# Four gathers of 4 KB rows in place of one gather of 16 KB rows, in a chain of adapter and paged-attention layers

## The chip, the cores and the metric

The kernel runs on one core of one Trainium2 chip. The metric is the device time of one execution in microseconds (us). The five engines are called PE (TensorE), DVE (VectorE), ACT (ScalarE), POOL (GpSimd) and SP (SyncE); PEld is PE's loading of weights. POOL issues all indirect transfers (gathers and scatters); SP and ACT issue the plain ones.

## The reference

The input is 64 batches of 64 tokens with 512 features. Four residual layers follow one another:

```python
x = x + einsum('bct,bcd->bdt', x, weights[conditions])            # layer 0
x = x + x @ W_base.T + lora(x, adapter_idx)                       # layer 1
x = x + attention(x, k_blocks, v_blocks, block_tables, kv_lens)   # layer 2
x = x + x @ W.T + lora2(x, adapter_idx)                           # layer 3
```

Layer 2 matters here. It projects queries, keys and values, normalises and rotates queries and keys, writes the 64 new keys and values of each batch into blocks of a paged cache, and attends over a window of 256 positions:

```python
slot, off = pos // 16, pos % 16
blk = take_along_axis(block_tables, slot, axis=1)
k_blocks = k_blocks.at[blk, :, off, :].set(k)
v_blocks = v_blocks.at[blk, :, off, :].set(v)
k_all, v_all = k_blocks[block_tables], v_blocks[block_tables]
o = softmax(mask(q @ k_all.T * SCALE)) @ v_all
```

A block holds 16 positions, 4 key heads and 64 numbers for each: 4,096 floats, 16 KB. The block tables are drawn at random, so a batch may see blocks that another batch has written.

## The kernel before, in words

The work has two loops, and the order of all instructions is written out by hand: each engine runs its own in the order in which the program issues them.

The **first loop** (L879 on, 39 rounds) does layers 0 and 1 and the projections for tiles of 128 tokens. The new keys and values of each tile are scattered by POOL (`put_rows`, L831) into two tables in DRAM, `pk` and `pv`. These hold one row of 4,096 floats for each of the 5 blocks that a batch writes (64 x 5 = 320 rows); in a row the 16 positions come one after the other, each with 4 heads of 64. Before, the rows were filled with the old blocks, so that a row of `pk` is a whole block with the new tokens in it. Index lists are made in rounds 13 to 20: `ik_old` and `ik_new` for keys, `iv_old` and `iv_new` for values. An index of `ik_new` names the row of `pk` that a block of the window has become, or lies beyond the last row if nobody wrote that block; a gather skips such indices.

The **second loop** (L1117) has 128 steps, 8 to each group `q` of four batches; `i` is the step within the group, and each step does two key heads of one batch. A group's window is 21 blocks for each of four batches, so its keys stand on 84 partitions. They come about in four moves:

- `k_load` (L148): two gathers of old blocks into `kt`, 84 rows of 8 KB each, at steps 2 and 3, two groups ahead.
- `k_copy` (L154): four copies of `kt` into `k2`, which turns (head, position) into (position, head). Three of them run at steps 5 to 7, on DVE (ACT for the first two groups), the last on ACT at step 0.
- `k_patch` (L161): one gather from `pk` over `k2`, 84 indices, rows of 16 KB. It is issued at step 1 for the next group (L1130), and for group 0 at the end of the first loop (L896).
- `k_turn` (L169): PE transposes `k2` in eight turns of four (`psk` in the profile), one at step 3 and the others until step 7; ACT and DVE copy the outcome into `kT_mem`, from which the scores are made. A turn reads one position out of each quarter of the block: positions `o4`, 4 + `o4`, 8 + `o4` and 12 + `o4`.

Values go a like way: `v_load` (four gathers of 92 rows of 1 KB, in every even step), `v_copy` on ACT, `v_patch` (L199, one gather of 92 indices from `pv`, rows of 4 KB, in every odd step), and `v_share`, three small transfers on SP's queue that wait for the patch.

At a step POOL is given, in this order: at an odd step the value patch, then at step 1 the key patch; at an even step the four value loads; at steps 2 and 3 an old-key load. In the first 8 steps POOL also does the last multiplication of the remaining query tiles (`turned`, L218, the row L248), which PE transposes two steps later (`turn_q`, L276, `pst`). Where the first loop goes over to the second (round 32, L895 to L899) the order is: key patch of group 0, value patches of batches 0 and 1, then the multiplication of a query tile.

In the profile `k2` is named `k`, so the key patch is `k<-pk,ik_new`, the old-key load `kt<-in_kblk_dram,ik_old`, the value load `vs_mem<-in_vblk_dram,iv_old` and the value patch `vt_mem<-pv,iv_new`. All gathers are issued by the helper `gather` and have its line, L65.

Of the kernel before, what the change touches and what calls it, by code (L numbers as in the profile page):

```python
# [11 lines left out]
I32 = mybir.dt.int32  # L12
AF = mybir.ActivationFunctionType
ALU = mybir.AluOpType
# [4 lines left out]
P = 128  # L19
B, T, D = 64, 64, 512  # L20
# [3 lines left out]
NB_TAB = 257  # L24
# [7 lines left out]
NR = 21  # L32
NW = 5
W0 = NR - NW
NWR = B * NW
# [15 lines left out]
def kernel(  # L51
# [9 lines left out]
    V, S, G, PE, DMA = nc.vector, nc.scalar, nc.gpsimd, nc.tensor, nc.sync  # L61

    def gather(dst, src, idx, bound=None):
        more = {} if bound is None else dict(bounds_check=bound, oob_is_err=False)
        G.indirect_dma_start(  # L65
            out=dst, out_offset=None, in_=src,
            in_offset=bass.IndirectOffsetOnAxis(ap=idx, axis=0), **more,
        )
# [19 lines left out]
    pk = dram.tile([NWR, ROW], F32, name="pk", tag="pk")  # L88
# [4 lines left out]
    def ctile(shape, dt, name, pool=const):  # L93
        return pool.tile(shape, dt, name=name, tag=name)
# [14 lines left out]
    woT_sb = ctile([P, 4, D], F32, "woT_sb")  # L109
# [7 lines left out]
    edge = ctile([P, 1], F32, "edge")  # L117
    lowb = ctile([P, B], F32, "lowb")
    ik_old = ctile([4 * NR, 2, 16], I32, "ik_old")
    ik_new = ctile([4 * NR, 16], I32, "ik_new")  # L120
    iv_old = ctile([NV, B, NG], I32, "iv_old")
    iv_new = ctile([NV, B], I32, "iv_new")
    iod_f = iod.rearrange("p o q j -> p (o q j)")
# [8 lines left out]
    k2 = ctile([P, BLK, NG, HD], F32, "k2")  # L132
# [8 lines left out]
    def bank(pool, name):  # L141
        return pool.tile([P, 512], F32, name=name, tag="b")

    NP = 4 * NR
# [13 lines left out]
                k2[:NP].rearrange("p (oq o) g d -> p oq o g d", o=4)[:, :, o4],  # L158
                kt[:NP].rearrange("p g (oq o) d -> p oq o g d", o=4)[:, :, o4])

    def k_patch(q):  # L161

        if q < B // 4:
            gather(k2[:NP].rearrange("p o g d -> p (o g d)"), pk, ik_new[:, q : q + 1], NWR - 1)

    def kT(q, gp):
        return kT_mem[q % 2][:, gp].rearrange("p (b o c i) -> p b o c i", b=4, o=3, c=4)
# [31 lines left out]
    def v_patch(b):  # L199
        if b < B:  # L200
            gather(vt_mem[:NV, b % 4], pv.rearrange("w (q r) -> (w q) r", q=4),
                   iv_new[:, b : b + 1], NWR * 4 - 1)
# [11 lines left out]
    def queries(n):  # L214

        return n - LQ if n < NTILE - 4 else -1 if n < NTILE else n - 4 - LQ
# [77 lines left out]
    with ExitStack() as one:  # L294
# [4 lines left out]
        def t1(shape, dt, name):  # L299
            return ctile(shape, dt, name, c1)  # L300
# [41 lines left out]
                        for i in range(2))  # L342
        kvb_i = t1([P, B], I32, "kvb_i")
        kvp_i = t1([P, 1], I32, "kvp_i")
        cond_i = t1([P, B], I32, "cond_i")
        ad1_i = t1([P, B], I32, "ad1_i")
        ad3_i = t1([P, B], I32, "ad3_i")
        tab_i = woT_sb[:, 2, :NB_TAB].bitcast(I32)
        sc1b = t1([P, 4], F32, "sc1b")
        sc3b = t1([P, 8], F32, "sc3b")  # L350
        pcol = t1([P, 1], F32, "pcol")
# [212 lines left out]
        def gather_indices(part):  # L564

            ps = bank(psO, f"ps_idx{part}")
            lhs, rhs, m, n = ((ix["lhs"].rearrange("p b j -> p (b j)"), ix["hi"], 4 * NR, 16)
                              if part < 2 else
                              (ix["lhsv"].rearrange("p c i -> p (c i)")[:, :NV], ident2, NV, B))
            o = ps[:m, :n]  # L570
            PE.matmul(o, lhsT=lhs, rhs=rhs, start=True, stop=True)
            if part == 0:
                for h in range(2):
                    V.tensor_scalar(ik_old[:, h], o, 2.0, float(h), ALU.mult, ALU.add)
            elif part == 1:
                V.tensor_copy(ik_new, o)
            elif part == 3:
                V.tensor_scalar(iv_new, o, 4.0, ix["oq"], ALU.mult, ALU.add)
            else:
                for g in range(NG):  # L580
                    V.tensor_scalar(iv_old[:, :, g], o, 16.0, ix["oqg"][:, g : g + 1],
                                    ALU.mult, ALU.add)
# [299 lines left out]
        for n in range(NLAST):  # L882
# [10 lines left out]
                put_rows(done["p"])  # L893
                done["p"] += 1
            if n == NTILE:  # L895
                k_patch(0)  # L896
                v_patch(0)
                v_patch(1)
                norm_q(queries(n - 1))()  # L899
# [217 lines left out]
    for s, (q, b, gp) in enumerate(steps):  # L1117
        i = s % 8
        turn1, turn2 = turns.get(i, (None, None))
        if i == 0 and q:  # L1120
            x_load(q)
        if i == 2:
            q_load(q + 1)
        if gp == 0:
            v_load(b + 3)
        else:
            v_share(b + 1)
            v_patch(b + 2)
        if i == 1:
            k_patch(q + 1)  # L1130
        if i in (2, 3):
            k_load(q + 2, i - 2)
        scores(s + 1)
        turn_p(s)
        if 0 < s < 16:
            turn_q(nq + s - 2, psO)
        if turn1:
            k_turn(q + 1, *turn1)
        maxima(s + 1)
        keep_p(s)  # L1140
        exponentials(s + 1)
        second = norm_q(nq + s if q < 2 else -1)
        if parts:
            parts.pop(0)()
        if q < 2:
            product_q(nq + s + 1, psM)
            x2_load(nq + s + 3)
        shares(s + 1)
        second()
        if gp:  # L1150
            window(b + 2)
        po = values(s)
        if turn2:
            k_turn(q + 1, *turn2)
        keep_o(s, po)
        if gp == 0:
            v_copy(b + 2)
        if i == 0:
            k_copy(q + 1, 3)
        elif i > 4:  # L1160
            k_copy(q + 2, i - 5)
        if i == 7:
            parts += last_parts(q)
# [53 lines left out]
```

## Time and profile before

| what | us |
|---|---|
| median of 14 runs | 1233.82 |
| lowest and highest of them | 1220.99, 1244.74 |
| the profiled execution's own time | 1228.75 |
| its span, first to last instruction | 1227.0 |
| granted TensorE clock, mean | 0.979 |

The profile is of one execution. A busy time is the sum of an engine's instructions; issuing a plain transfer doesn't count as busy, but a gather's work on POOL does, and a transfer goes on in the DMA engines after POOL has done with it. A row of a timeline gives the start, the duration, the engine, the line, the operation with what it writes and reads, how many are merged, and in brackets how long the engine stood idle before and what ended that: an instruction of another engine, a transfer (DMA), or "issue", where nothing that the profile shows was waited for. The chain of waits follows back, from the last instruction, what each step was released by. The landing of a gather is read from the records of its semaphore, which counts the sixteen DMA engines that have finished their part; in the second loop some of these records are missing, so that a landing read there is the latest that is known.

### The profile page before, as it was taken

The page shows a single profiled execution, that of the slowest core. Times are in us where ns is not written, and L with a number is a line of the kernel's source. Part 1 is how long each engine was busy: PE and PEld are TensorE (multiplying, and loading weights), DVE is VectorE, ACT ScalarE, POOL GpSimd, SP SyncE. Part 2 cuts the span into 40 slices and gives each one's busy share as a digit, 9 for nine tenths or more (in the row PEclk, how much of TensorE's full clock was granted, in tenths as well). Part 3 has the DMA queues.
Part 4 walks back from the last instruction along what each step waited for, and adds up shares of the span by engine and source line. Part 5 has one row for each costly group of instructions (what it writes and reads, how often), then busy time and mean ns, then how long its engine had stood idle before and what let it go on. Part 6 is the DMA issues. An engine that isn't in the chain of part 4 may idle for free.

```text
span 1227.0 us, 17686 instructions
## 1 busy us (share of the span) xinstructions
PE 1103.7 (90%) x5622; PEld 636.9 (52%) x5622; DVE 755.4 (62%) x2313; ACT 571.7 (47%) x1472; POOL 612.3 (50%) x601
## 2 busy tenths in 40 slices
PE   4899899999999968978999998898999799999998
PEld 3434444444444434446555555655665555665565
DVE  3775346766666655885665665665666465666561
ACT  1332222232324324545665665565665465666651
POOL 3243323332642442887566656656666556665520
PEclk9999899999999988999999999999999899999999
DMA  8365713234331363636456645645656645755420
GB/s 268 133 250 209 237 41 113 90 97 132 113 110 47 108 181 110 167 93 153 133 134 142 148 121 129 155 120 124 163 134 136 142 120 126 157 143 143 98 64 35
DMA packets 129820, 163.20 MB, mean 133 GB/s; under 512 B 58079, under 2 KB 96891, under 8 KB 125545
## 3 DMA queue, kind: packets, MB, share of 16 engines
q0 software_dynamic: 63872, 85.04, 28.7%
q1 hardware_dynamic: 46416, 53.89, 14.5%
q10 hardware_dynamic: 19440, 23.15, 5.6%
q8 instruction: 45, 0.74, 0.3%
q14 instruction: 47, 0.39, 0.1%
HBM read 139.66 MB, written 50.33 MB: 155 GB/s over the span
## 4 chain that ended last, share of the span: by engine, by line
PE 68%; DVE 9%; issue 7%; DMA 6%; ACT 4%; POOL 2%; another core or an unknown queue 0%; ACTq 0%; POOLq 0%; DVEq 0%; SPq 0%
PE pso L1059 9%; PE pp L1025 8%; PE po L1041 7%; PE psc L983 7%; PE q L263 6%; PE ps L787 5%; PE kv L820 5%; PE psy L1084 4%; PE psy L1078 4%; PE psk L175 4%; PE psxa L1067 2%; PE psy L1086 2%; PE ps L789 2%; DMA pk<-vt_mem,zidx 1%; PE pst L283 1%
## 5 line engine op out<-in xcount | busy, mean ns | idle before, releaser
L65 POOL DMA_INDIRECT vs_mem<-in_vblk_dram,iv_old x256 | 310.5, 1213 | 77.4 <-issue 69.8
L65 POOL DMA_INDIRECT vt_mem<-pv,iv_new x64 | 80.1, 1252 | 168.1 <-ACT vt_mem L197 87.1
L1009 ACT ACTIVATE sm_mem<-sm_mem,mn 128x336 f32<-128x336 f32 x256 | 145.6, 574 | 32.9 <-DVE mn L999 28.4
L999 DVE CUSTOM_DVE_ANT_0 sm_mem<-psc,pen 128x336 f32<-128x336 f32 x256 | 119.5, 500 | 46.0 <-PE pp L1025 21.8
L1041 PEld LDWEIGHTS po<-pT,vt_mem 124*64 124x64 f32 x1536 | 84.5, 137 | 87.4 <-ACT sm_mem L1009 53.8
L1041 PE MATMUL po<-pT,vt_mem 124*64 124x128 f32 x1536 | 117.6, 282 | 13.1 <-issue 7.1
L1059 PE MATMUL pso<-oT,woT_sb 128*128 128x256 f32 x512 | 123.2, 385 | 0.0
L263 PE MATMUL q<-wq_sb,x2q 128*128 128x512 f32 x256 | 121.1, 618 | 0.0
L1025 PE MATMUL pp<-ident,sm_mem 128*124 128x128 f32 x768 | 115.0, 282 | 6.6 <-DVE rsum L1016 3.3
L820 PE MATMUL kv<-wkv_sb,xr 128*128 128x512 f32 x256 | 118.1, 606 | 0.4 <-ACT va L828 0.4
L983 PE MATMUL psc<-kT_mem,qs 64*128 64x336 f32 x512 | 108.0, 497 | 10.8 <-DVE kT_mem L184 9.7
L1025 PEld LDWEIGHTS pp<-ident,sm_mem 128*124 128x124 f32 x768 | 80.8, 139 | 70.7 <-issue 59.4
L787 PE MATMUL ps<-kT_mem,kT_mem 128*128 128x512 f32 x256 | 115.3, 593 | 0.6 <-PE ps_fill L493 0.6
L1017 DVE TENSOR_SCALAR sm_mem<-sm_mem,rsum 128x336 f32<-128x336 f32 x256 | 107.4, 420 | 9.1
L248 POOL TENSOR_TENSOR q<-q,rsq 128x512 f32<-128x512 f32 x30 | 31.4, 1048 | 138.8 <-DVE rsq L246 108.1
L1059 PEld LDWEIGHTS pso<-oT,woT_sb 128*128 128x128 f32 x512 | 92.5, 192 | 12.6 <-ACT pen L973 2.1
L175 PE MATMUL psk<-ident,k 84*128 84x84 f32 x512 | 63.8, 251 | 29.5 <-ACT kT_mem L184 13.6
L1032 DVE COPY pT<-pp 124x384 f32<-124x384 f32 x128 | 70.7, 552 | 18.6 <-PE pp L1025 6.8
L263 PEld LDWEIGHTS q<-wq_sb,x2q 128*128 128x128 f32 x256 | 50.1, 200 | 59.6 <-issue 59.4
L787 PEld LDWEIGHTS ps<-kT_mem,kT_mem 128*128 128x128 f32 x256 | 48.4, 190 | 60.5 <-issue 59.3
L820 PEld LDWEIGHTS kv<-wkv_sb,xr 128*128 128x128 f32 x256 | 47.9, 194 | 58.1 <-issue 56.4
L1032 ACT COPY pT<-pp 124x384 f32<-124x384 f32 x128 | 61.6, 482 | 34.1 <-PE pp L1025 25.4
(223 smaller groups left out, 1742.3 us busy)
## 6 DMA issues: line engine op xcount, KB each, us to landing
xt<-in_x_dram SPq DMA_DIRECT2D x32, 256.0 KB
x2d<-xr SPq DMA_DIRECT2D x8, 1024.0 KB
x2q<-x2d SPq DMA_DIRECT2D x32, 256.0 KB
qd<-qt ACTq DMA_DIRECT2D x64, 128.0 KB
qs<-qd SPq DMA_DIRECT2D x16, 512.0 KB
xq<-x2d SPq DMA_DIRECT2D x16, 512.0 KB
out_dram<-ys ACTq DMA_DIRECT2D x32, 256.0 KB
vt_mem<-vt_mem SPq DMA_DIRECT2D x192, 28.0 KB
```

Of the source, the lines that this page charges most:

```text
L65: G.indirect_dma_start(out=dst, out_offset=None, in_=src, in_offset=bass.IndirectOffsetOnAxis(ap=idx, axis=0), **more,)
L175: PE.transpose(ps[:, oq, :], k2[:NP, 4 * oq + o4, 2 * gp : 2 * gp + 2].rearrange("p g d -> p (g d)"), ident[:NP, :NP])
L263: PE.matmul(psq[n], lhsT=xt[:, c, :], rhs=wq_sb[:, c, :], start=(c == 0), stop=(c == KC - 1))
L787: PE.matmul(ps, lhsT=wb_sb[:, c, oc * P : (oc + 1) * P], rhs=x1_mem[:, c, :], start=(c == 0), stop=False)
L820: PE.matmul(pskv[n], lhsT=xrs[s][:, c, i * P : (i + 1) * P], rhs=wkv_sb[:, c, :], start=(c == 0), stop=(c == KC - 1))
L983: PE.matmul(pscs[s][g], lhsT=qts[q][gs, gp, b % 4].rearrange("p h t -> p (h t)"), rhs=kT(q, gp)[gs, b % 4].rearrange("p o c i -> p (o c i) ...
L999: V.tensor_tensor_reduce(rows4(sm)[:, :, :, :28], rows4(pscs[s][g]), rows4(pens[b]), SCALE, 3.0e38, ALU.add, ALU.min, mn)
L1009: S.activation(w, w, AF.Exp, bias=mn, scale=-1.0, accum_out=rsum)
L1025: PE.transpose(pp[:NVK, o, :], sms[s][g][0][:, o * P : o * P + NVK], ident)
L1032: (V.tensor_copy if g else S.copy)(pT, pps[s][g][:NVK])
L1041: PE.matmul(po[g * HD : (g + 1) * HD, :], lhsT=vt(b)[:NVK, o, 2 * gp + g], rhs=pTs[s][g][:, o, :], start=(o == 0), stop=(o == 2))
L1059: PE.matmul(o, lhsT=woT_sb[:, c, ec * P : (ec + 1) * P], rhs=oT[:, c // 2, :, c % 2, :], start=(c == 0), stop=(c == 3))
```

## The change

The gather of `k_patch` becomes four, each for a quarter of the 16 positions. `pk` is read as a table of 1,280 rows of 4 KB; the index of a quarter is four times the old index plus the quarter's number, and the bound is four times as large, so the same blocks are skipped. The index list grows from 16 to 64 numbers on a partition and is made by four DVE instructions in place of one. At both places the four are issued one after the other where the one stood. To make room, two index tables that are used only at the very start (`cond_i`, `ad1_i`) move into a part of `woT_sb` that is loaded later; another such table stood there already.

```diff
-    ik_new = ctile([4 * NR, 16], I32, "ik_new")
+    ik_new = ctile([4 * NR, 4, 16], I32, "ik_new")
...
-    def k_patch(q):
+    def k_patch(q, oq):
         if q < B // 4:
-            gather(k2[:NP].rearrange("p o g d -> p (o g d)"), pk, ik_new[:, q : q + 1], NWR - 1)
+            gather(k2[:NP, 4 * oq : 4 * oq + 4].rearrange("p o g d -> p (o g d)"),
+                   pk.rearrange("w (q r) -> (w q) r", q=4), ik_new[:, oq, q : q + 1], NWR * 4 - 1)
...
-        cond_i = t1([P, B], I32, "cond_i")
-        ad1_i = t1([P, B], I32, "ad1_i")
         ad3_i = t1([P, B], I32, "ad3_i")
-        tab_i = woT_sb[:, 2, :NB_TAB].bitcast(I32)
+        tab_i, cond_i, ad1_i = (woT_sb[:, 2, lo : lo + n].bitcast(I32)
+                                for lo, n in ((0, NB_TAB), (NB_TAB, B), (NB_TAB + B, B)))
...
             elif part == 1:
-                V.tensor_copy(ik_new, o)
+                for oq in range(4):
+                    V.tensor_scalar(ik_new[:, oq], o, 4.0, float(oq), ALU.mult, ALU.add)
...
             if n == NTILE:
-                k_patch(0)
+                for oq in range(4):
+                    k_patch(0, oq)
                 v_patch(0)
                 v_patch(1)
                 norm_q(queries(n - 1))()
...
         if i == 1:
-            k_patch(q + 1)
+            for oq in range(4):
+                k_patch(q + 1, oq)
```

## The prediction

> **What bounds the kernel now.** I read the page first, then the busy time by stage, then POOL's timeline around the gathers that change, then the chain of waits and the records of DMA packets and landings. All times are of the one profiled execution.
>
> ```profile
> span 1227.0 us, 17686 instructions
> ...
> PE 1103.7 (90%) x5622; PEld 636.9 (52%) x5622; DVE 755.4 (62%) x2313; ACT 571.7 (47%) x1472; POOL 612.3 (50%) x601
> ```
>
> PE is busy 90% and POOL, which issues the changed gathers, 50%. The average hides stages, so here are three: the change-over from the first loop to the second, the first attention period with its leftover query work, and the rest. Columns: stretch, its length, busy time (instructions) of PE, PEld, DVE, ACT, POOL, granted clock, DMA share, GB/s.
>
> ```profile
> 445.00:475.00 30.00, 16.79 (x65) 10.39 (x66) 10.30 (x26) 8.05 (x22) 9.32 (x9) 0.74 0.46 129
> 475.00:545.00 70.00, 59.70 (x308) 31.90 (x307) 58.14 (x139) 38.70 (x101) 53.06 (x46) 0.94 0.48 128
> 545.00:1190.00 645.00, 592.10 (x3895) 380.05 (x3896) 398.85 (x1342) 386.69 (x1035) 390.53 (x330) 0.99 0.56 133
> ```
>
> In the last, PE leads (592 of 645). In the second, POOL's 53 us of 70 leave out about 0.3 us of issue before each gather. In the first no engine is busy: something is waited for. POOL's timeline there, then PE's row (start, duration, what, idle time and releaser):
>
> ```profile
> 445.97 0.97 POOL L71 DMA_INDIRECT pk<-k,sidx  x1 [0.30 <-issue]
> 449.22 1.03 POOL L65 DMA_INDIRECT k<-pk,ik_new  x1 [2.27 <-DMA pk<-k,sidx]
> 450.55 1.28 POOL L65 DMA_INDIRECT vt_mem<-pv,iv_new  x1 [0.31 <-issue]
> 452.14 1.24 POOL L65 DMA_INDIRECT vt_mem<-pv,iv_new  x1 [0.30 <-issue]
> 453.40 2.05 POOL L248 TENSOR_TENSOR q<-q,rsq 128x512 f32<-128x512 f32 x2
> ```
> ```profile
> 454.51 1.12 PE L283 MATMUL pst<-ident,q 128*128 128x128 f32 x4 [10.71 <-POOL q L248]
> ```
>
> The key gather (k<-pk) waits for the last new key rows to land, two value gathers and the query products queue behind it on POOL, and PE, DVE and ACT all stand still (10.7, 11.5 and 11.8 us) until the first product is done. Whatever POOL issues between 449.2 and 453.4 is on the path.
>
> **The change, part by part.**
>
> *Price of one gather.* The 16 key gathers take 1.012 us each on POOL; the old-key gather with the same 84 indices and half the bytes takes 0.966 (32 of them), so the time follows the indices, not the bytes. A quarter has 84 indices: 1.01 us, bounded by 0.97 and the 1.25 of the value gather with 92 indices. With 0.30 us of issue a gather costs 1.32 us (736.39 to the next start, 737.71). Three more each time: 3.95 us, sixteen times.
>
> *Change-over: +3.95 us.* The three stand ahead of both value gathers and the query products. Nothing hides them, and the rows after 454.5 depend on PE's transposes, so all shifts.
>
> *First period: +2.36 us.*
>
> ```profile
> 498.98 1.02 POOL L65 DMA_INDIRECT k<-pk,ik_new  x1 [0.30 <-issue]
> 500.08 0.24 POOL L242 TENSOR_SCALAR rsq<-rsq 128x8 f32<-128x8 f32 x1
> ...
> 513.03 1.04 POOL L248 TENSOR_TENSOR q<-q,rsq 128x512 f32<-128x512 f32 x1
> ```
> ```profile
> 515.70 0.63 PE L283 MATMUL pst<-ident,q 128*128 128x128 f32 x4 [0.99 <-issue]
> ```
>
> From 487.9 to 546 POOL's rows follow one another with only issue gaps, so 3.95 us at 499 are carried along. Pairing the products with PE's transposes in order, the slack is 4.7 us for the next one (503.20 to 507.86) but 1.63 us for the one after (514.07 to 515.70): PE gets it at 518.02, 2.36 us late. The following slacks (2.5, 2.3 us) are then covered. At 547.8 POOL again waits for DVE (1.31 us) and the lag is gone. Bounds: 0, if other engines' slack takes it, and 3.95.
>
> *Fourteen steady periods (44.6 us each): POOL's time is hidden.*
>
> ```profile
> 734.86 1.23 POOL L65 DMA_INDIRECT vt_mem<-pv,iv_new  x1 [3.38 <-PE pp L1025]
> 736.39 1.01 POOL L65 DMA_INDIRECT k<-pk,ik_new  x1 [0.30 <-issue]
> 737.71 1.21 POOL L65 DMA_INDIRECT vs_mem<-in_vblk_dram,iv_old  x1 [0.30 <-issue]
> ...
> 745.50 1.24 POOL L65 DMA_INDIRECT vt_mem<-pv,iv_new  x1 [0.86 <-issue]
> ...
> 757.57 1.23 POOL L65 DMA_INDIRECT vt_mem<-pv,iv_new  x1 [3.45 <-DMA vt_mem<-vt_mem]
> ```
>
> Behind the three stand four value loads, the first old-key load, a value patch, the second key load and four more value loads; the idle 0.86 and 3.45 us take the lag back by 757.6. Their readers are later: values loaded from 737.7 land by 748 and are copied by ACT at 756.2; the patch of 745.5 ends in SP's three sharing DMAs at 753.8 to 755.5, read by PE at 766.3; the second key load (747.1) lands by about 755.7 and DVE copies it at 763.0. The thinnest margin, landing to key copy, is 4.9 us (889.9 to 894.8), over 3.95. If that cover fails it costs under 1 us in a period.
>
> *The landing of the key gather itself* is what PE's first key transposes (psk) wait for.
>
> ```profile
> 691.27 11.02 DMA k<-pk,ik_new
> ```
>
> This piece of the chain of waits is one gather from its issue to its landing; PE idled 0.82 us for it. From the landings' semaphore records, PE waits 0.82, 1.04 and 0.25 us in periods 5, 14 and 15: 2.1 us to win, no more. Two more landings are under 0.7 us ahead of PE, one 2.1, the others 3.8 or more (many landings lack records, so these margins are upper bounds). Why so late? Each gather moves about 37 of 84 rows (599 packets of 16,384 bytes over 16 gathers; the others are skipped), each 1.06 us in the median, and one DMA engine takes several in turn: the gather of 449.22 finds the rings nearly empty and still lands at 457.98, 8.8 us later. Now the quarters: packets of 4,096 bytes on this queue have a median of 0.16 us and a mean of 0.27, so four cost 0.64 to 1.08 against 1.06. The first quarter starts when the whole did and the rings are fed for 3.95 us longer; an engine with five rows needs 5.3 us now, and 3.95 + 5 x 0.16 to 0.27 = 4.8 to 5.3 us then. That is nowhere later. Bounds: -2.1 us (no wait left) and, if the whole landing slips with the last issue by 3.95 us, the sum of 3.95 less each period's margin where positive: 0.1 + 3.95 + 3.55 + 1.83 + 0.05 + 3.35 + 3.95 + 2.91 = 19.7 us. I take 0, near the lower end, because 8.8 us of landing against 1.0 of issue says that packets, not issue, set it.
>
> A rule speaks against the change. The Trainium skill, "DMA: Bandwidth & Descriptors", section "Anatomy of one DMA — SWDGE (gpsimd) path", fits a DMA at 2.0 us plus bytes over 436 GB/s, and its rules for kernel authors say to coalesce small transfers. As an estimate from that page, the whole (613 KB) would land 3.4 us after issue and a quarter 2.4, so the last quarter would come 2.9 us later than the whole, which with the margins above is 13.2 us of PE waits and a total near 1253. The trace has 7.7 us after POOL's end at 450.25, not 3.4, so I let the packets decide.
>
> *The rest.* Three more index instructions on DVE of 0.12 us (the row is 117 ns) near 250 us, in a stage where PE is busy 285 of 299 us: nothing, or 0.35 us uncovered. PE waits for four semaphores instead of one, on four transposes that are there anyway. The two index tables that move into another tile are loaded and read in the first microseconds: nothing.
>
> *Sum.* 3.95 + 2.36 + 0 + 0 = 6.3 us. The profiled execution took 1228.75 (span 1227.0): 1235.1 after it. That execution is 5.1 us under the median of the 14 runs, so against 1233.82 I say 1240. A measurement of this kernel tells about 0.5%, 6.2 us, from no change; the forecast stands on that edge.
>
> **The rivals.**
>
> *The last quarter lands late (slower).* PE's fourth transpose waits for the last quarter. For it: six landings stand within 2.1 us of PE. Against it: packets set the landing. At 2 us later the waits are 2.0 + 1.6 + 1.4 + 2.0 + 1.0 = 8.0 us: 1248; the whole bound gives 1260.
>
> *Half the price (no change).* Shorter packets take away the 2.1 us of waits and the first period's lag goes into PE's idle (10 us of 70): 3.95 - 2.1 = +1.9, 1236. For it: 0.16 us is the median. Against it: PE is issued in order there and the slack was read row by row.
>
> *Long packets hold up everything else (faster).* Place: the rings in the fourteen steady periods, where a 16 KB packet keeps an engine for 1.06 us while SP's sharing DMAs and the value loads wait; with them gone, landings come sooner and PE's 53 idle us of 645 shrink. It decides from 0.45 us a period (6.3 / 14). At 1 us a period: 6.3 - 14 = -7.7, 1226. Against it: readers have 5 to 10 us of slack, and PE's waits that name a DMA there are few.
>
> **How the numbers follow.** Forecast 0.54, with its own range 1237.5 to 1243 (unknowns of the first period and landing); late quarter 0.18; half price 0.18; faster 0.10. Of the forecast I put 0.32 above the 0.5% and 0.22 below. Slower 0.32 + 0.18 = 0.50; same 0.22 + 0.18 = 0.40; faster 0.10. The range 1230 to 1252 leaves out most of the faster case and the upper part of the late one, under 0.2 together.
>
> **What would show it.** Right: four k<-pk rows of about 1.0 us in the change-over and PE's idle before the first pst near 14.7 us; in the first period a PE wait of some 2 us for POOL's product; psk waits of at most 2 us in all; steady periods of 44.6 us. Wrong: psk waits of a microsecond in most periods (late quarter), steady periods under 44.1 us (long packets), or quarters that take POOL far from 1.0 us.

## The result, and the profile after

The changed kernel takes 1353.22 us in the median of 10 runs (1337.21 to 1360.80), the kernel before 1234.25 in the median of 47 (1220.99 to 1249.03, but for two at 1582.83 and 3108.73). The ratio is 1.094, 95% interval 1.090 to 1.098, of the means of the runs that lie within 1.5% of the fastest of their kernel: 9% slower, where 1240 was forecast with a range up to 1252. The page of the profiled execution (1341.83 us, mean granted clock 0.931 against 0.979):

```profile
span 1340.1 us, 17856 instructions
...
PE 1155.8 (86%) x5622; PEld 671.4 (50%) x5622; DVE 754.8 (56%) x2316; ACT 573.0 (43%) x1472; POOL 660.5 (49%) x649
...
PEclk9999899998999788889989979789899899898999
```

TensorE does the same 5,622 matmuls in 52 us more, and is idle 61 us more. The slices show why it is busier: of the last twenty, eight have a granted clock of 7 or 8 tenths, where the kernel before had a single 8. The three stages (columns as in the prediction):

```profile
445.00:475.00 30.00, 13.46 (x46) 6.90 (x44) 9.66 (x20) 4.64 (x12) 12.66 (x12) 0.77 0.48 146
475.00:545.00 70.00, 55.05 (x267) 30.36 (x268) 50.07 (x125) 35.48 (x91) 46.30 (x41) 0.87 0.40 111
545.00:1190.00 645.00, 552.16 (x3348) 353.14 (x3350) 348.10 (x1158) 335.39 (x893) 383.59 (x331) 0.91 0.48 118
```

In the third, 3,348 matmuls are done in 645 us where 3,895 were, and no engine is busier than TensorE with its 86%: every one does less in the same time. **Where the 113.1 us of span came from**, read from the start of the first key gather, the starts of ACT's copies of the attention result (`oT<-po`, one a step) and the end: 3.5 us were there before the first key gather was issued (it starts at 452.7 against 449.2; over all executions here, it starts anywhere between 447.9 and 456.6, so this is scatter), 3.9 us in the change-over, 6.3 us in the first attention period, 99.5 us in the fourteen steady periods (7.1 us each, 51.3 in place of 44.2), nothing in the last.

So the loss is a steady-period loss. One period, timeline of all engines (start, duration, what, idle before and releaser):

```profile
770.71 1.02 POOL L65 DMA_INDIRECT k<-pk,ik_new  x1 [0.30 <-issue]
...
773.39 0.24 ACT L1051 COPY oT<-po 128x128 f32<-128x128 f32 x1
...
774.64 1.00 POOL L65 DMA_INDIRECT k<-pk,ik_new  x1 [0.30 <-issue]
...
774.91 0.88 PE L1043 MATMUL po<-pT,vt_mem 124*64 124x128 f32 x12
...
775.71 0.83 PE L985 MATMUL psc<-kT_mem,qs 64*128 64x336 f32 x4
...
780.82 0.27 ACT L1051 COPY oT<-po 128x128 f32<-128x128 f32 x1 [5.68 <-PE pso L1061]
...
782.25 0.51 DVE L1001 CUSTOM_DVE_ANT_0 sm_mem<-psc,pen 128x336 f32<-128x336 f32 x1 [4.40 <-remote]
...
784.31 1.62 PE L1043 MATMUL po<-pT,vt_mem 124*64 124x128 f32 x12 [4.07 <-issue]
```

The same place in the kernel before:

```profile
736.39 1.01 POOL L65 DMA_INDIRECT k<-pk,ik_new  x1 [0.30 <-issue]
...
739.07 0.24 ACT L1049 COPY oT<-po 128x128 f32<-128x128 f32 x1
...
740.61 0.88 PE L1041 MATMUL po<-pT,vt_mem 124*64 124x128 f32 x12
...
743.95 0.27 ACT L1049 COPY oT<-po 128x128 f32<-128x128 f32 x1 [3.14 <-PE pp L1025]
```

The values product of step 2 (`po`) is shown from 774.91 to 775.79, and what it waits for, pieces from ACT and DVE and landed transfers, is there. Yet ACT, which waits for this product and for nothing else, gets it at 780.82, 5 us after its end as shown; DVE gets the scores (`psc`), whose row ends at 776.54, at 782.25, 5.7 us late. The trace also records the updates of the semaphore by which TensorE says that a result is there: 780.79 for this product, 782.23 and 782.27 for the scores. So it is not ACT or DVE that is slow to look: TensorE reports its results later than its rows say, and a row's end is modelled, not measured. Whether TensorE works late or only its report is late no record shows; that the reports come 1.4 us apart, and not all at once, speaks for the work. What ACT and DVE hand to TensorE is taken at once. Then TensorE has nothing to do (4.07 us), and its clock is halved from 783.0 on, for 13.7 us (the column behind the busy times):

```profile
783.00:784.00 1.00, 0.00 (x0) 0.00 (x0) 0.42 (x3) 0.22 (x1) 0.77 (x1) 0.52 0.69 127
784.00:785.00 1.00, 0.69 (x6) 0.69 (x8) 0.33 (x1) 1.00 (x4) 0.70 (x2) 0.50 0.55 164
```

I call **lag** the time from the shown end of the product (or of ACT's own work before it, if that is later) to ACT's copy. At step 2 it is 1.84 us before and 4.96 after, in the mean of the fifteen periods with a key gather; at all other steps it is under 0.15 in both. Half-clock time in the fourteen steady periods is 7 us before and 123 after, in stretches of mostly 3.4, 6.8 and 13.7 us. Together: 15 x 3.12 = 47 us of lag, and at most half of the 116 us at half speed, 58: 105, an upper estimate for the 99.5.

### The profile page after: what moved, and what is told of

Its sections match the earlier page's. It is cut to its first block, busy times and chain, and to the rows that moved or that the text cites. A ratio compares the mean times of both kernels' runs of the same rounds, so it can differ in the third digit from the quotient of the medians.

```text
span 1340.1 us, 17856 instructions
## 1 busy us (share of the span) xinstructions
PE 1155.8 (86%) x5622; PEld 671.4 (50%) x5622; DVE 754.8 (56%) x2316; ACT 573.0 (43%) x1472; POOL 660.5 (49%) x649
## 4 chain that ended last, share of the span: by engine, by line
PE 65%; DVE 8%; issue 7%; DMA 6%; POOL 4%; ACT 4%; another core or an unknown queue 3%; ACTq 0%; POOLq 0%; DVEq 0%; SPq 0%
PE pso L1061 8%; PE pp L1027 8%; PE po L1043 8%; PE psc L985 7%; PE ps L788 5%; PE psy L1080 4%; PE q L264 4%; PE psy L1086 4%; PE psk L176 4%; PE kv L821 4%; PE psxa L1069 3%; PE psy L1088 2%; DMA pv<-vt_mem,zidx 2%; PE ps L790 1%
## 5 line engine op out<-in xcount | busy, mean ns | idle before, releaser
L1043 PE MATMUL po<-pT,vt_mem 124*64 124x128 f32 x1536 | 125.5, 290 | 52.5 <-ACT pT L1034 40.2
L1043 PEld LDWEIGHTS po<-pT,vt_mem 124*64 124x64 f32 x1536 | 89.4, 140 | 128.5 <-ACT pT L1034 47.5
L1027 PE MATMUL pp<-ident,sm_mem 128*124 128x128 f32 x768 | 122.6, 296 | 17.7 <-issue 14.9
L1027 PEld LDWEIGHTS pp<-ident,sm_mem 128*124 128x124 f32 x768 | 86.6, 146 | 87.1 <-issue 72.0
L985 PE MATMUL psc<-kT_mem,qs 64*128 64x336 f32 x512 | 115.7, 529 | 10.3 <-DVE kT_mem L185 10.3
L821 PE MATMUL kv<-wkv_sb,xr 128*128 128x512 f32 x256 | 115.4, 595 | 0.4 <-ACT va L829 0.4
L1051 ACT COPY oT<-po 128x128 f32<-128x128 f32 x128 | 33.8, 264 | 153.5 <-PE po L1043 67.4
L176 PE MATMUL psk<-ident,k 84*128 84x84 f32 x512 | 70.4, 269 | 32.4 <-ACT kT_mem L185 16.3
```

Of the source, the lines that this page charges most:

```text
L176: PE.transpose(ps[:, oq, :], k2[:NP, 4 * oq + o4, 2 * gp : 2 * gp + 2].rearrange("p g d -> p (g d)"), ident[:NP, :NP])
L821: PE.matmul(pskv[n], lhsT=xrs[s][:, c, i * P : (i + 1) * P], rhs=wkv_sb[:, c, :], start=(c == 0), stop=(c == KC - 1))
L985: PE.matmul(pscs[s][g], lhsT=qts[q][gs, gp, b % 4].rearrange("p h t -> p (h t)"), rhs=kT(q, gp)[gs, b % 4].rearrange("p o c i -> p (o c i) ...
L1027: PE.transpose(pp[:NVK, o, :], sms[s][g][0][:, o * P : o * P + NVK], ident)
L1043: PE.matmul(po[g * HD : (g + 1) * HD, :], lhsT=vt(b)[:NVK, o, 2 * gp + g], rhs=pTs[s][g][:, o, :], start=(o == 0), stop=(o == 2))
```

## The experiments

Each set of kernels ran on one chip, with the kernel before beside them; the five sets fell on five chips. Single runs, but for the last kernel (median of 4) and the kernel before in set 5 (median of 7). "Lag" is the mean of the fifteen periods with a key gather (of the same places where there is none), "period" the mean of periods 1 to 14, from result copy to result copy, both of the one profiled execution.

| kernel | set | us | before beside it | lag, step 2 | period |
|---|---|---|---|---|---|
| four quarters, nothing moved | 1 | 1347.24 | 1247.85 | 4.54 | 51.7 |
| whole gather, nothing moved | 1 | 1229.58 | 1247.85 | 2.04 | 43.7 |
| whole gather, POOL busy behind it | 1 | 1261.91 | 1247.85 | 0.16 | 46.1 |
| one quarter only | 1 | 1229.17 | 1247.85 | 2.06 | 43.8 |
| no key gather | 2 | 1192.26 | 1197.70 | 0.05 | 41.4 |
| two halves | 2 | 1193.80 | 1197.70 | 0.05 | 41.4 |
| four, all rows in range | 2 | 1222.10 | 1197.70 | 0.05 | 42.9 |
| four, taken apart | 2 | 1264.17 | 1197.70 | 0.05 | 46.2 |
| the changed kernel again | 3 | 1361.98 | 1235.60 | 4.56 | 52.6 |
| two halves again | 3 | 1275.78 | 1235.60 | 2.62 | 47.3 |
| no key gather again | 3 | 1229.23 | 1235.60 | 0.05 | 43.8 |
| small packets from SP | 3 | 1244.02 | 1235.60 | 1.97 | 44.7 |
| four of 96 indices | 4 | 1325.43 | 1249.38 | 6.41 | 50.3 |
| four of 92 indices | 4 | 1301.41 | 1249.38 | 0.24 | 48.3 |
| before, key and old-key gathers of 96 | 4 | 1240.27 | 1249.38 | 2.42 | 44.6 |
| before, all gathers of 96 | 4 | 1391.88 | 1249.38 | 0.26 | 55.4 |
| four, paced | 5 | 1263.14 | 1238.00 | 0.06 | 45.7 |
| before, paced | 5 | 1212.71 | 1238.00 | 0.06 | 43.6 |

### Set 1: is it the rows, the gathers, or POOL's time?

**Four quarters that move nothing.**

```diff
-                    V.tensor_scalar(ik_new[:, oq], o, 4.0, float(oq), ALU.mult, ALU.add)
+                    V.tensor_scalar(ik_new[:, oq], o, 4.0, SKIP, ALU.mult, ALU.add)
```

> The four quarter gathers are issued as in the changed kernel, but all their indices lie beyond the bound, so that no new key row is moved: new keys are left out of the attention. The question is where the 5.1 us come from by which the values product of step 2 is late in every period of the changed kernel (1.8 us before). Theory A (rows: 4 KB rows being written to the key tile hold up TensorE): nothing is moved, the lag is gone, the time is 1230 us or less. Theory B (gathers: it is the number of gathers with their skipped rows, each of which still makes a packet of 4 bytes): there are more skipped rows than ever, the lag stays 5 us or more, the time about 1340. Theory C (place: the 3.95 us by which POOL issues the value and old-key loads later): POOL's rows are as in the changed kernel, the lag stays, 1340.

1347.24 us, lag 4.54: everything is as in the changed kernel. ACT's row at step 2 of one period, of this kernel's timeline:

```profile
735.28 0.27 ACT L1051 COPY oT<-po 128x128 f32<-128x128 f32 x1 [5.97 <-PE pso L1061]
```

The 5.97 us are there without a single new row on its way. Theory A, and with it every reading by the new rows' bytes, their packets of 4 KB or their landing, falls.

**The whole gather, moving nothing.**

```diff
-                V.tensor_copy(ik_new, o)
+                V.tensor_scalar(ik_new, o, 1.0, SKIP, ALU.mult, ALU.add)
```

> The kernel before with all indices of its one key gather beyond the bound, so that no new key row is moved: new keys are left out. Theory A: the 1.8 us of lag in each of fourteen periods goes too, 1205 to 1215 us. Theories B and C: nothing changes by more than 0.5%, 1225 to 1235, and the lag stays near 1.8 us.

Lag 2.04, 1229.58: as B and C said. The kernel before has the same trouble in small, and not from its rows.

**POOL kept busy behind the whole gather.**

```diff
             k_patch(q + 1)
+            for _ in range(4):
+                G.tensor_tensor(dl, dl, dl, ALU.mult)
```

> The kernel before with one whole key gather, and behind it, in each period, four POOL multiplications of 128x512 (about 1.04 us each by the row of the query product), which write a tile that nobody reads. All that POOL issues behind them comes some 4.2 us later, as in the changed kernel. Theory C: the lag of step 2 grows to about 5 us and the time to about 1340. Theories A and B: the lag stays at 1.8 us and the time within 10 us of 1234.

Nobody's number: the lag is gone (0.16), and C, which wanted 5 us, falls. The time is 14 us over the kernel before all the same: step 1 takes 8.3 us instead of 5.8 in nearly every period, and 7.1 instead of 5.7 in the last, which has no key gather, so that is the price of the multiplications. What they do besides is put 4 us between the key gather and the gathers behind it. I did not see then what that meant.

**One quarter of four.**

```diff
         if i == 1:
-            for oq in range(4):
+            for oq in range(1):
                 k_patch(q + 1, oq)
```

> The changed kernel with only the first of the four quarter gathers in each attention period (all four stay at the change-over): three quarters of the new keys are left out from group 1 on. POOL's rows are as before the change, a quarter of the data is moved, in rows of 4 KB. Theory A: the lag is about a quarter of 5.1 us, 1.3, and the time near 1230. Theory B: one gather with its skipped rows as before the change, lag 1.8 us, 1235. Theory C: no shift, lag 1.8 us or less, 1235. If 4 KB rows hold up TensorE more than 16 KB rows for the same bytes, the lag is above a quarter of what the changed kernel has.

Lag 2.06, 1229.17: like one whole gather with four times its bytes. B and C both allow it, A does not.

### Set 2: how many gathers? A chip without the lag

**No key gather in the periods; two halves; four with all rows in range; four taken apart.** The edits:

```diff
-        if i == 1:
-            for oq in range(4):
-                k_patch(q + 1, oq)
```
```diff
-            gather(k2[:NP, 4 * oq : 4 * oq + 4].rearrange("p o g d -> p (o g d)"),
-                   pk.rearrange("w (q r) -> (w q) r", q=4), ik_new[:, oq, q : q + 1], NWR * 4 - 1)
+            gather(k2[:NP, 8 * oq : 8 * oq + 8].rearrange("p o g d -> p (o g d)"),
+                   pk.rearrange("w (q r) -> (w q) r", q=2), ik_new[:, oq, q : q + 1], NWR * 2 - 1)
```
```diff
+            src, bound = ((kblk.rearrange("n g o d -> (n g) (o d)"), NBLK * 4 - 1) if q else
+                          (pk.rearrange("w (q r) -> (w q) r", q=4), NWR * 4 - 1))
...
+                for oq in range(4):
+                    V.tensor_scalar(ik_new[:, oq, 1:], o[:, 1:], 4.0, float(oq), ALU.mult, ALU.add)
```
```diff
             for g in range(NG):
                 gather(vs_mem[:NV, b % 2, g].rearrange("p o d -> p (o d)"), v_rows,
                        iv_old[:, b, g : g + 1])
+                if b > 3 and b % 4 == 0 and g < 3:
+                    k_patch(b // 4, g + 1)
```

> The changed kernel with no key gather at all in the attention periods (the four of the change-over stay): new keys are left out from group 1 on. Dose zero. If the key gathers themselves, by their number, make the values product of step 2 late (theory B, now the leading one, since four gathers that move nothing cost the same 112 us as four that move rows), the lag is 0.1 us, periods are about 42 us and the time is 1200 to 1215 us. If any long row of gathers does it (value and old-key loads too: theory D), half a microsecond to 1.5 us of lag stays and the time is 1220 to 1230.

> Two gathers of 8 KB rows in place of four of 4 KB, everywhere. Theory B: one gather gives 1.8 us of lag and four 5.1, so two give 2.9 by a straight line, and of the 112 us a third, 1265 to 1275. If there is a threshold instead (a lag only when more descriptors are queued than something holds), two could stay at 1.8 us and 1237, or jump to 5 us and 1340.

> The changed kernel, but in the attention periods the four gathers take rows of 4 KB from the table of old blocks, with all 84 indices in range: no row is skipped, 1.4 MB instead of 0.6 MB is moved in a period, and old keys in another order of positions and heads stand in the place of the new ones. If skipped rows make the lag (theory B in its narrow form), it falls under 1 us, and the time to 1240 or less unless the bytes cost something. If the gathers do it with or without skipping, the lag stays at 5 us and the time at 1340 or above.

> The changed kernel with the four gathers of a period taken apart: the first stands where it stood, the other three each behind one of the next value loads (value, key, value, key, value, key, value). POOL's total work, the rows and the bytes are those of the changed kernel. If it is the key gathers' number, the lag of 5 us and 1340 stay. If it is that they come one directly behind the other, the lag falls towards 1.8 us and the time to 1240 to 1270. Key transposes may wait for the last quarter, which is issued some 4.6 us later: up to 4 us a period against a margin of 7 to 10.

The set can't answer its question: on this chip the kernel before took 1197.70 us, below all 47 runs of the result, and none of the four kernels has a lag. What it does tell: no key gather and two halves are the same (41.4 us a period, 1192 and 1194), so without lag the gathers of a period are hidden, two of them at least, as the prediction reasoned for POOL. Both are below every forecast (1200 to 1230; 1237 and more), which counted on a chip with the lag. The other two fall where their forecasts allow (1240 or less; 1240 to 1270), but a kernel without lag says nothing of what takes a lag away. Four gathers with all rows in range (1.4 MB) make TensorE's key transposes wait 12.0 us in all for landings between 560 and 1170 us; the four taken apart, which issue the last quarter 4.5 us later, 33.0 us:

```profile
PE psk L178 <- DMA k<-in_kblk_dram,ik_new: 12.0, 15, 1.4
```
```profile
PE psk L176 <- DMA k<-pk,ik_new: 33.0, 18, 2.7
```

Another thing sets this chip apart: its traces are all but whole. The trace of two halves holds 14,209 records of the transfers' semaphores here and 10,543 in set 3.

### Set 3: the same kernels on a chip with the lag

The changed kernel, two halves and no key gather are unchanged; the fourth is the kernel before with

```diff
         keep_o(s, po)
+        if i == 1:
+            for j in range(3):
+                DMA.dma_start(out=tiny[:, 3 * q + j : 3 * q + j + 1],
+                              in_=oTs[q][:, gp, b % 4, 0, j : j + 1])
```

> The changed kernel once more, beside the following three on one chip. In the second set the kernel before took 1197.7 us where it took 1221 to 1249 in all runs up to then, no kernel of that set had a late values product (0.05 us at step 2), and the trace had all its semaphore records, of which those with the lag lack a third, most of them just while TensorE is late. Theory R (the record of the execution itself: gathers make packets and semaphore events, each is written down, and where that writing is saturated records are lost and TensorE, which has the most to write, is held up): lag and loss of records come together. On a chip with loss: 1335 to 1360 us, lag 5 us. On one without: no lag, 1195 to 1210. Theory G (the gathers hold TensorE up as such): lag 5 us and 1335 to 1360 on any chip.

> The two gathers of 8 KB rows once more (1193.8 in the second set, against 1197.7 for the kernel before on that chip). On a chip with lag and lost records: between one gather and four, 2.9 us of lag and 1255 to 1285. On one without: equal to before within 0.5%. Theory G would have a lag on either.

> No key gather in the attention periods (new keys left out from group 1 on), once more. On a chip with lag and lost records: lag near zero and 1195 to 1210 if the key gathers' packets are what fills the record to the brim; 1.8 us and 1225 if other transfers do that alone. On one without: 1192 as in the second set.

> The kernel before, and in each period, after the first odd step, three transfers on SP's queue of 128 packets of 4 bytes each (1.5 KB in all, from the result tile to a DRAM table that nobody reads): about as many packets and semaphore events as three more gathers with their skipped rows make, but no gather, no work on POOL, and next to no bytes. Theory R: on a chip with loss of records, the lag at steps 2 and 3 grows from 1.8 us by 1 to 4 us a period, 1250 to 1310; on one without, 1198 to 1205. Theory G: the lag stays as in the kernel before and the time within 0.5% of it on any chip.

The changed kernel is back at 1361.98 with a lag of 4.56, and two halves lie between: 2.62 us, 1275.78, where the chip of set 2 had 1193.80 from the very same instructions. ACT's copies at steps 1 and 2 of one period of two halves, first on the chip of set 2, then of set 3:

```profile
690.45 0.25 ACT L1051 COPY oT<-po 128x128 f32<-128x128 f32 x1
692.90 0.27 ACT L1051 COPY oT<-po 128x128 f32<-128x128 f32 x1 [0.70 <-PE po L1043]
```
```profile
707.53 0.24 ACT L1051 COPY oT<-po 128x128 f32<-128x128 f32 x1
712.38 0.27 ACT L1051 COPY oT<-po 128x128 f32<-128x128 f32 x1 [3.11 <-PE pp L1027]
```

2.45 us from copy to copy against 4.85. With none, one, two and four gathers the lag is 0.05, 1.8 to 2.1, 2.6 and 4.5 to 5.0: it goes with their number, and theory G, which wanted it on any chip, falls. The small packets brought 0.13 us of lag and 8 us of time, far from the 1 to 4 us a period of theory R: three transfers of 128 small packets a period, on SP's queue, are not enough.

The kernel without key gathers missed its time: 1195 to 1210 was named for a lag near zero, and it took 1229.23, 6 us less than the kernel before beside it. Its steps 3 and 4 take 13.5 us together from copy to copy, where the same instructions took 11.1 on the chip of set 2. In the steady periods ACT and DVE take up 66 of TensorE's results there more than 0.5 us after the shown end and after their own last row, all but three of them at steps 3 and 4, behind the two gathers of old keys. In each of the four kernels of set 2 it is one. So the key gather is not alone in making TensorE late; the lag at step 2 sees only what happens behind the key gather.

### Set 4: is it the number of indices?

The index lists get twelve (or eight) more entries beyond the bound; for the quarters:

```diff
-    ik_new = ctile([4 * NR, 4, 16], I32, "ik_new")
+    ik_new = ctile([96, 4, 16], I32, "ik_new")
...
-            gather(k2[:NP, 4 * oq : 4 * oq + 4].rearrange("p o g d -> p (o g d)"),
+            gather(k2[:96, 4 * oq : 4 * oq + 4].rearrange("p o g d -> p (o g d)"),
...
+                G.memset(ik_new, 1 << 20)
                 for oq in range(4):
-                    V.tensor_scalar(ik_new[:, oq], o, 4.0, float(oq), ALU.mult, ALU.add)
+                    V.tensor_scalar(ik_new[: 4 * NR, oq], o, 4.0, float(oq), ALU.mult, ALU.add)
```

> The changed kernel with twelve more indices in each key gather, all beyond the bound (96 in place of 84; the rows moved are the same). Theory S (shape: 84 indices leave two of sixteen DMA engines without rows, and such gathers hold TensorE up): 96 goes evenly, the lag falls from 4.5 to 5.1 us to under 1, the time to 1235 or less on a chip with lag. Theory N (number: any gather put in this place, whatever its indices): lag 4.5 us or more, 1335 to 1365. On a chip without lag both give 1195 to 1215.

> The same with eight more indices (92, the number of the value gathers, which in rows of five make no lag). A gather of 92 takes 1.2 us of POOL in place of 1.0 and leaves some 270 more packets of 4 bytes. Theory S in the form that 84 is what hurts and 92 not: lag under 1 us, 1235 to 1250. Theory N, and the record's theory R all the more, since there are more packets to write down: lag 5 us or more, 1340 to 1400.

> The kernel before with its key gather and its two old-key loads at 96 indices (twelve more, all beyond the bound). Theory S: the lag of 1.8 us at step 2 and what steps 3 and 4 take beyond 6.1 and 5.0 us go, 1195 to 1210 on a chip with lag, so faster than the kernel before. Theory N: 1225 to 1250 as before.

> The same, and the value gathers (four loads and a patch per batch) at 96 indices in place of 92. If an even spread makes fewer packets (92 leave about 270 packets of 4 bytes each) and POOL's time per gather falls from 1.2 us towards 1.05, POOL's work falls by some 40 us in all, which is hidden in the periods. Theory S: at or under the time of the kernel with only the key gathers padded. Theory R: the fewer packets, the less lag, so under it too. Theory N: as the kernel before.

96 indices do not take the lag away (6.41 and 2.42; the kernel before with them took 1240.27, as theory N said), so an uneven 84 is not the cause. 92 take the lag at step 2 away (0.24), though part of the loss comes back at later steps (48.3 us a period), and 1301.41 us is what no theory had named. And all gathers of 96 indices, expected to be the best, are the worst of all, at 1391.88: TensorE is late at most steps (by the count above, 133 results in the steady periods against 103 in the kernel before, though not the one behind the key gather, lag 0.26), with 23,472 packets of gathers in the second loop against 55,952. Its steady stage:

```profile
560.00:1170.00 610.00, 492.52 (x2907) 315.07 (x2908) 294.44 (x994) 292.87 (x773) 247.82 (x252) 0.89 0.38 108
```

Both shape (S) and packets (R) fail here. What fits the lag in all of them is in POOL's rows. A gather of 84 or 96 indices takes POOL 0.95 to 1.02 us, one of 92 takes 1.2. With 0.3 us of issue they start 1.3 or 1.5 us after one another. Value gathers, in rows of five, are 1.5 apart and without lag; the quarters are 1.3 apart and TensorE is late behind them; of 92 indices, 1.5 apart, and it is not late at step 2; and when value gathers have 96, 1.3 apart, TensorE is late behind them too:

```profile
830.84 0.97 POOL L65 DMA_INDIRECT vs_mem<-in_vblk_dram,iv_old  x1 [0.30 <-issue]
832.11 0.98 POOL L65 DMA_INDIRECT vs_mem<-in_vblk_dram,iv_old  x1 [0.31 <-issue]
```

### Set 5: the pace

Shape, number and rows stay; a POOL operation on 128x8 numbers goes behind each key gather of a period:

```diff
             for oq in range(4):
                 k_patch(q + 1, oq)
+                G.tensor_scalar(tick, tick, 1.0, None, ALU.mult)
```
```diff
             k_patch(q + 1)
+            G.tensor_scalar(tick, tick, 1.0, None, ALU.mult)
         if i in (2, 3):
             k_load(q + 2, i - 2)
+            G.tensor_scalar(tick, tick, 1.0, None, ALU.mult)
```

> The changed kernel, and behind each quarter gather of a period one POOL operation on 128x8 numbers (0.24 us by the row of the query scale, about 0.3 with its gap), so that gathers start 1.6 us after one another instead of 1.3. Theory P (pace: gathers that start 1.3 us apart are faster than something behind them takes them, the backlog holds TensorE up; 1.5 us apart they do not): lag under 1 us, 1235 to 1260 on a chip with lag. Theory S (shape: rows over 14 or 16 DMA engines): lag 4.5 us or more, 1335 to 1365. On a chip without lag both give 1195 to 1215.

> The kernel before with the same operation behind its one key gather and behind each of the two old-key loads. Theory P: the 1.8 us of lag at step 2 and the excess of steps 3 and 4 go, 1200 to 1215 on a chip with lag, faster than the kernel before by 2%. Theory S: 1230 to 1240, the same as the kernel before. On a chip without lag 1197 to 1202 either way.

The quarters now start 1.5 us apart (707.89, 709.39, 710.94), and ACT gets the product of step 2 after 0.74 us of idling instead of 5.68, in this kernel's timeline:

```profile
707.89 1.01 POOL L65 DMA_INDIRECT k<-pk,ik_new  x1 [0.30 <-issue]
708.94 0.25 POOL L1136 TENSOR_SCALAR tick<-tick 128x8 f32<-128x8 f32 x1
709.39 1.06 POOL L65 DMA_INDIRECT k<-pk,ik_new  x1 [0.20 <-issue]
...
713.01 0.27 ACT L1051 COPY oT<-po 128x128 f32<-128x128 f32 x1 [0.74 <-PE po L1043]
```

Some 0.2 us more between gathers that are otherwise the same, and the lag is 0.06 us instead of about 5, the time 1263.14 (theory P: 1235 to 1260) instead of 1337 to 1362. TensorE's report for this product is recorded at 712.99, where its row ends at 712.97. The unpaced quarters were not run on this chip; that it is one with the lag is read from the 1238.00 of the kernel before, from the traces of the two paced kernels, which lack semaphore records as the others do, and from the results taken up late in them, 89 and 67 by the count above, where set 2 had one. At step 2 theory P holds and S falls. It is still 25 us over the kernel before: the four of the change-over are not paced, POOL's work is longer, and steps 4 to 7 take 3.5 us a period more than before. The two old-key loads, which are not paced in this kernel and are followed by the next gather after 1.25 us, come just before those steps; I did not follow that up.

In the kernel before, the same few operations pay. Median 1212.71 us (4 runs, 1205.95 to 1220.54) against 1238.00 (7 runs), ratio 0.979, interval 0.971 to 0.986: faster than both kernels, by 1.4 to 2.9%, and this comparison is within one chip. ACT's copies at steps 1 and 2 are 2.52 us apart where they were 4.88 in the trace of the kernel before, and the clock has no 8 in the steady periods:

```profile
PEclk9999899999999988999999999999999999999999
...
738.60 0.25 ACT L1049 COPY oT<-po 128x128 f32<-128x128 f32 x1
...
741.12 0.27 ACT L1049 COPY oT<-po 128x128 f32<-128x128 f32 x1 [0.78 <-PE po L1041]
```

Half of this forecast missed. Theory P wanted the excess of steps 3 and 4 to go as well, since the old-key loads are paced here too:

```profile
743.50 0.94 POOL L65 DMA_INDIRECT kt<-in_kblk_dram,ik_old  x1 [0.30 <-issue]
744.47 0.26 POOL L1136 TENSOR_SCALAR tick<-tick 128x8 f32<-128x8 f32 x1
744.93 1.27 POOL L65 DMA_INDIRECT vt_mem<-pv,iv_new  x1 [0.20 <-issue]
```

At 1.43 us from start to start it stays: steps 3 and 4 take 13.1 us together, against 12.1 in the trace of the kernel before and 11.1 on the chip of set 2, and 58 of the 67 results taken up late are there.

**What stays open.** Shown: on the chips of the result and of sets 1, 3 and 4, and not on that of set 2, key gathers make TensorE late at step 2, whatever they move, when the next gather starts 1.3 us behind each; at 1.5 us, by 92 indices (set 4) or by a POOL operation in between (set 5), they don't. Not shown: that pace is all there is to it, since behind the old-key loads TensorE is late at 1.43 us too; what lies behind POOL that takes a gather in about 1.5 us, if that is what it is; and why TensorE stands still for it. That the chip decides is read from one set on each chip. The chip without lag is also the one whose traces lost hardly any semaphore records; but the paced kernel before lost as many as the unpaced one (10,083 records kept against 10,289) with hardly a lag at step 2 left, so loss of records and lag are companions on a chip, and neither is shown to make the other. The Trainium skill, "NOTIFIC — the notification-queue block", section 7.1 (Overflow: three behaviours, one of which stalls the engine), says that the block which writes trace records away can hold up the engine that produces them. That would make part of the lag a cost of being recorded; every time here is of a recorded execution, so no run can tell.

## Why the prediction was wrong, point by point

*Price of one gather: right.* Four rows of 1.00 to 1.04 us, 1.31 to 1.34 from start to start.

*Change-over: right, +3.95.* From the first key gather to the query product it is 8.13 us now (452.68 to 460.81), where it was 4.18, and TensorE's idle time before the first `pst` is 14.53, where 14.7 was named:

```profile
452.68 1.03 POOL L65 DMA_INDIRECT k<-pk,ik_new  x1 [2.27 <-DMA pk<-k,sidx]
...
460.81 2.05 POOL L249 TENSOR_TENSOR q<-q,rsq 128x512 f32<-128x512 f32 x2
...
461.91 1.11 PE L284 MATMUL pst<-ident,q 128*128 128x128 f32 x4 [14.53 <-POOL q L249]
```

*First period: right in kind, too small.* TensorE waits for POOL's product as forecast, 4.03 us where some 2 were named:

```profile
525.84 1.11 PE L284 MATMUL pst<-ident,q 128*128 128x128 f32 x4 [4.03 <-POOL q L249]
```

The period cost 6.3 us, not 2.36 (2.32 by the rows that the prediction gives, 515.70 to 518.02), and more than its upper bound of 3.95. That it is longer is no scatter: it takes 69.6 to 72.4 us in all kernels with four gathers, also on the chip without lag, and 64.5 to 68.5 in those with none to two (the one with POOL kept busy aside). The excess over 3.95 may be: the means are 71.2 with four gathers and 66.8 with one, 4.3 apart.

*Fourteen steady periods, "POOL's time is hidden": the step that failed.* POOL's own time was hidden: its readers were not late, and without lag a second gather cost nothing (set 2). But the step took for granted that a gather has no effect except its time on POOL and its landing. It has a third: gathers at 1.3 us make TensorE late, 3.3 us more a steady period, and the halved clock behind that costs at most 4.1 more. The term that the sum put at 0 was 99.5 us: 7.1 in each period, where "if that cover fails it costs under 1 us in a period" stood. The trace of before showed the effect, in the row at 743.95 above: ACT idle for 3.14 us behind a product whose row had ended 2.46 us earlier, and the like in thirteen of the fifteen periods that have a key gather, just behind it. I read POOL's slack and the landings, and not that row.

*The landing of the key gather: right, with luck.* In the change-over, where all records are there, the last quarter landed 8.7 us after the first issue, the whole before 8.8: nowhere later, as forecast, though not in the 4.8 to 5.3 us that the sum over packets gave. No wait of TensorE's transposes in the steady stage names the key gather, but that is no test, since TensorE comes to them late itself, 12 to 17 us after the first quarter's issue in place of 9.5 to 11.4; the last known records of the last quarter are 6 to 8 us after it. The paced quarters are a fairer one: there TensorE comes after 8 to 10 us, the last known records are 8 to 9 us after the issue, and no wait names the key gather either. The 13.2 us of the prediction's estimate by the page are not there. The Trainium skill says elsewhere, "SBUF — State Buffer", section "Who interferes with whom", where it is about the memory's ports, that TensorE waits on no one and that transfers never contend with a compute engine. The trace agrees as far as data goes, since quarters that move nothing cost the same. TensorE's results are 3 to 7 us late all the same; whether a port has a part in that no run shows.

*The rivals.* Late quarter: no; it appears only where the quarters move all their rows (12.0 us) or are taken apart (33.0 us). Half the price: no. Long packets: no; shorter ones gained nothing. None of the rivals had TensorE's own delay in it, because the question was put only to POOL and to the queues. The range was too narrow for the same reason: its ends were sums of waits that I could name.

## What to carry to other kernels

Count gathers by their pace as well as by their time: where several follow each other on POOL, look at what the other engines' results do just then, and try a small POOL operation between them before blaming bytes or landings. When a consumer starts microseconds after the shown end of TensorE's product and waits for nothing else, TensorE was late, whatever its row says, and a stall of some 4 us can be paid a second time through the clock, as at 783.0 here; the 2 us of the kernel before hardly were (7 us of half clock in fourteen periods). Measure a change on more than one chip before giving it a price.

## What was not expected of the hardware

- TensorE's results came 3 to 7 us after their shown end, with no wait open, behind key gathers that POOL issued 1.3 us apart; at 1.5 us apart the lag was 0.06 us.
- The same two-halves kernel took 1193.80 us on one chip and 1275.78 on another; the kernel before 1197.70 on the one and 1235.60 to 1249.38 on the other four.
- Half-clock stretches followed the lag: 123 us of them in the fourteen steady periods, against 7.
- Gathers of 96 indices take POOL less time than gathers of 92 (1.00 against 1.21 us) and make fewer than half the packets (112 against 384); with them in all places the kernel went from 1249.38 to 1391.88 us.
- Three POOL operations of 0.25 us a period, which put off what follows by some 0.2 us each, made the kernel before 2% faster.
